# Moving the Wv projection and the transposes of x1 on TensorE in a GCN and graph attention kernel

## Chip, cores, metric

One core of one Trainium2 chip. The metric is the device time of one launch in microseconds, correct against the reference. Kernels are compared in rounds on the same chip.

## The reference, cut to what matters

64 graphs of 256 nodes with 512 features, float32. Two layers, each with a residual and a layer norm:

```python
# layer 0: three graph convolutions
h = relu(adj @ (x @ W1) + b1)
h = relu(adj @ (h @ W2) + b2)
x1 = layernorm(x + adj @ (h @ W3) + b3)
# layer 1: graph attention with one weight per node
q, k = split(x1 @ Wqk); v = x1 @ Wv
w = softmax(mask * sum(q * (adj @ (k * mask)), -1) / sqrt(512))   # over the nodes
out = layernorm(x1 + w[:, :, None] * v)
```

## The kernel before

It works on pairs of graphs in a software pipeline: while pair i goes through layer 0, pair i-1 goes through the end of layer 0 and through the attention. A 512x512 projection takes seven products of half size in place of eight (a Strassen scheme); the sums of the left side are made by VectorE and GpSimd. Wq and Wk are folded into one matrix Wm. A scheduler orders the instructions of each engine; the order of the source is only its starting point.

```python
def left(src, own, eng1, eng2, name, bufs=1):     # sums ahead of a projection
    ...
    eng1.tensor_tensor(S1, A21, A22, op=OP.add)
    eng2.tensor_tensor(S3, A11, A21, op=OP.subtract)
    eng1.tensor_tensor(S2, S1, A11, op=OP.subtract)
    eng2.tensor_tensor(S4, A12, S2, op=OP.subtract)

def seven(lf, w, dst, nodes_out):                 # X, Y, W, Z are PSUM banks
    # X = A11 B11; Y = A12 B21; X += S2 T2; W = S3 T3; X += S1 T1; Z = S4 B22; W += A22 N4
    # ScalarE copies X after the 1st, 3rd and 5th product, VectorE makes the four results
    ...

def load_rest(i):
    ...
    nc.sync.dma_start(xt, xn[i])
    ...
    nc.gpsimd.tensor_tensor(xt..., xt..., bl3..., op=OP.add)      # the bias add, L72

def layernorm(x, g):
    ...
    nc.vector.tensor_scalar(x[:, g, h, :], ..., op0=OP.subtract, op1=OP.mult)   # the scaling, L191

for i in range(NP + 1):
    new = i < NP
    if new:
        s = project(lx, w1, "s", 2)                          # W1
    if prev is not None:
        xt, an = rest
        layer0_out(prev, aTs[i - 1], xt)                     # pp, and the norm of layer 0: x1
    if new:
        ...
        hT = aggregate_relu(s, aTs[i], bl1)                  # pz: first adj product
    if prev is not None:
        x1T = transpose_x1(xt)                               # px: 16 transposes, 4 copies by ScalarE
    if new:
        s = project(left(hT, False, V, PL, "ch"), w2, "s", 2)    # h W2
        ...
    if prev is not None:
        l1 = left(x1T, True, V, PL, "c1")
        ...
        seven(l1, wm, ...)                                   # Wm -> yT
    if new:
        hT = aggregate_relu(s, aTs[i], bl2)                  # pz: second adj product
    if prev is not None:
        w = scores(i - 1, yT, x1T, an)                       # pg
    if new:
        s = project(left(hT, False, V, PL, "ch"), w3, "s", 2)    # h W3
    if prev is not None:
        sm = softmax_rows(w)                                 # pw
        v = project(l1, wv, "vs", 1)                         # x1 Wv
        layer1_out(i - 1, xt, v, softmax_cols(sm))           # ps; weighted v, norm, store
    if new:
        rest = load_rest(i)
    ...
    prev = s
```

## Time and profile before

| | before |
|---|---|
| time, median of 3 | 2982.35 us (2980.95 to 2983.51) |
| TensorE busy | 98% of the span |
| weight loads / VectorE / GpSimd / ScalarE busy | 82 / 46 / 23 / 22% |
| mean granted clock of TensorE, as a share of full speed | 0.996 |
| pass from pp to pp, mean of 29 | 91.57 us |

The page's busy shares say that TensorE is the bound. They do not say what it loses; for that one needs the list of TensorE's waits and the distance between equal points of the timeline. The prediction shows these lines.

How to read them: PE is TensorE's matmuls, PEld its weight loads, DVE VectorE, ACT ScalarE, POOL GpSimd. Numbers are left out of the program's names (c is c1; bx, by, bw, bz are the banks X, Y, W, Z), and x16 means 16 records. [0.53 <-DVE xt L191] means that the engine stood idle for 0.53 us until that instruction released it. An eviction copies a result out of PSUM, where the products are written. A pass is one turn of the loop, measured from pp to pp; the tail is what runs after the last pp.

### The profile page before, as it was taken

How to read it: one execution, taken by the hardware profiler on the slowest of the kernel's cores; microseconds unless marked ns; L12 is line 12 of the kernel's file. 1: busy time of each engine (PE TensorE's matmuls, PEld its weight loads, DVE VectorE, ACT ScalarE, POOL GpSimd, SP SyncE). 2: the span in 40 equal slices, each digit the busy share in tenths (PEclk: the TensorE clock that was granted, in tenths of full speed). 3: DMA queues.
4: the chain of work that ended last, by engine and by line, in shares of the span. 5: the costliest groups of instructions: out<-in, count | busy, mean ns of one | idle time of the engine just before them, and what ended most of it. 6: DMA issues, size and time to landing. Idle time of an engine off the chain costs nothing.

```text
span 2980.8 us, 32161 instructions
## 1 busy us (share of the span) xinstructions
PE 2926.8 (98%) x13216; PEld 2442.2 (82%) x13216; DVE 1363.5 (46%) x2386; ACT 661.5 (22%) x1130; POOL 698.1 (23%) x426
## 2 busy tenths in 40 slices
PE   8999999999999999999999999999999999999997
PEld 6788888888888888888888888888888888888885
DVE  3355334554345543455543455434555345554344
ACT  1222122222222222222212222222222122221221
POOL 4222022221222221222202222112222122221210
PEclk9999999999999999999999999999999999999998
DMA  5011101111011110111110111101111011111000
GB/s 195 22 61 61 46 25 57 53 61 60 11 60 50 60 61 26 45 57 54 60 54 18 60 50 60 61 11 60 50 61 60 32 39 57 53 60 50 8 29 28
DMA packets 33010, 151.29 MB, mean 51 GB/s; under 512 B 3680, under 2 KB 7904, under 8 KB 20320
## 3 DMA queue, kind: packets, MB, share of 16 engines
q1 hardware_dynamic: 32864, 149.24, 13.6%
q8 instruction: 104, 1.70, 0.2%
q14 instruction: 42, 0.34, 0.0%
HBM read 115.68 MB, written 33.55 MB: 50 GB/s over the span
## 4 chain that ended last, share of the span: by engine, by line
PE 90%; DVE 8%; DMA 1%; issue 1%; ACT 1%; POOL 0%; SPq 0%; DVEq 0%; POOLq 0%
PE bx L123 28%; PE bw L123 18%; PE pz L175 10%; PE bz L123 9%; PE by L123 9%; PE pg L223 7%; PE pp L199 6%; DVE xt L191 5%; DVE st L184 1%; PE px L212 1%; DVE xt L201 1%; DMA w<-in_W 1%; PE pt L302 0%; DMA xt<-in_xn 0%; DVE mv L185 0%
## 5 line engine op out<-in xcount | busy, mean ns | idle before, releaser
L175 PE MATMUL pz<-aT,s 128*128 128x256 f32 x2048 | 453.6, 379 | 0.0
L175 PEld LDWEIGHTS pz<-aT,s 128*128 128x128 f32 x2048 | 389.7, 190 | 66.7 <-issue 14.8
L109 POOL TENSOR_TENSOR hT<-hT 128x512 f32<-128x512 f32 x64 | 113.0, 1766 | 880.9 <-DVE ch L108 880.9
L108 POOL TENSOR_TENSOR cx<-xT 128x512 f32<-128x512 f32 x32 | 40.6, 1269 | 1024.9 <-DMA xT<-in_xT 990.0
L191 DVE TENSOR_SCALAR xt<-xt,mv,rs 128x512 f32<-128x512 f32 x256 | 276.8, 1123 | 1.2
L177 ACT ACTIVATE hT<-pz,bl 128x512 f32<-128x512 f32 x256 | 175.2, 685 | 400.8 <-PE pz L175 400.7
L123 PE MATMUL bw<-w,hT 128*128 128x256 f32 x1024 | 242.0, 379 | 1.6 <-POOL hT L109 1.6
L123 PE MATMUL bx<-w,ch 128*128 128x256 f32 x1024 | 242.0, 379 | 0.0
L153 DVE TENSOR_TENSOR s<-bw,t 128x512 f32<-128x512 f32 x96 | 66.4, 692 | 361.9 <-ACT t L152 361.9
L141 ACT COPY u<-bx 128x512 f32<-128x512 f32 x160 | 93.6, 585 | 612.7 <-PE bx L123 612.7
L223 PE MATMUL pg<-x1T,yT 128*128 128x256 f32 x1024 | 226.2, 379 | 0.0
L199 PE MATMUL pp<-s,aT 128*128 128x512 f32 x512 | 225.1, 592 | 0.0
L123 PEld LDWEIGHTS bw<-w,hT 128*128 128x128 f32 x1024 | 189.5, 190 | 33.4 <-POOL hT L109 2.0
L123 PEld LDWEIGHTS bx<-w,ch 128*128 128x128 f32 x1024 | 194.5, 190 | 26.6 <-issue 0.2
L223 PEld LDWEIGHTS pg<-x1T,yT 128*128 128x128 f32 x1024 | 194.6, 190 | 26.5
L152 ACT COPY t<-bx 128x512 f32<-128x512 f32 x160 | 93.6, 585 | 454.7 <-PE bx L123 447.4
L199 PEld LDWEIGHTS pp<-s,aT 128*128 128x128 f32 x512 | 97.2, 190 | 108.8 <-issue 107.1
L147 ACT COPY v<-bx 128x512 f32<-128x512 f32 x160 | 93.6, 585 | 406.5 <-PE bx L123 406.5
L184 DVE BATCH_NORM_STATS2 st<-xt 128x6 f32<-128x512 f32 x256 | 170.6, 688 | 2.1
L72 POOL TENSOR_TENSOR xt<-xt,bl 128x2048 f32<-128x2048 f32 x32 | 145.4, 4544 | 53.5 <-DMA xt<-in_xn 53.5
L108 DVE TENSOR_TENSOR ch<-hT 128x512 f32<-128x512 f32 x64 | 43.9, 686 | 234.5 <-ACT hT L177 234.5
L75 POOL TENSOR_TENSOR an<-an,mr 128x512 f32<-128x512 f32 x64 | 79.8, 1267 | 209.5 <-DMA an<-in_adjn 202.4
(108 smaller groups left out, 4543.2 us busy)
## 6 DMA issues: line engine op xcount, KB each, us to landing
xT<-in_xT SPq DMA_DIRECT2D x32, 1024.0 KB, 4.8
xt<-in_xn SPq DMA_DIRECT2D x32, 1024.0 KB, 6.9
out<-xt SPq DMA_DIRECT2D x32, 1024.0 KB, 3.9
aT<-in_adjT SPq DMA_DIRECT2D x32, 512.0 KB, 3.4
an<-in_adjn SPq DMA_DIRECT2D x32, 512.0 KB, 3.5
mr<-in_mask_row SPq DMA_DIRECT2D x32, 256.0 KB, 3.1
w<-in_W SPq DMA_DIRECT2D x9, 256.0 KB, 6.4
qT<-in_WqT SPq DMA_DIRECT2D x1, 1024.0 KB, 6.9
```

Source lines behind the costliest of these rows:

```text
L72: nc.gpsimd.tensor_tensor(xt.rearrange("p g h d -> p (g h) d"), xt.rearrange("p g h d -> p (g h) d"), bl3.unsqueeze(1).to_broadcast([P, G ...
L109: eng2.tensor_tensor(S3, A11, A21, op=OP.subtract)
L123: nc.tensor.matmul(bank[:, o], lhsT=lhsT, rhs=rhs, start=first and n == 0, stop=last and n == 3, skip_group_check=True)
L141: nc.scalar.copy(u, X)
L147: nc.scalar.copy(v, X)
L152: nc.scalar.copy(t, X)
L175: nc.tensor.matmul(pz[:, g, :], lhsT=s[:, g, m, f * P:(f + 1) * P], rhs=aT[:, g, m, :], start=(m == 0), stop=(m == NH - 1))
L177: nc.scalar.activation(hT[:, f], pz, AF.Relu, bias=bias[:, f:f + 1])
L184: nc.vector.bn_stats(st[:, h, :], x[:, g, h, :])
L191: nc.vector.tensor_scalar(x[:, g, h, :], x[:, g, h, :], mv[:, h, 0:1], rs[:, h:h + 1], op0=OP.subtract, op1=OP.mult)
L199: nc.tensor.matmul(pp, lhsT=aT[:, g, m, h * P:(h + 1) * P], rhs=s[:, g, m, :], start=(m == 0), stop=(m == NH - 1))
L223: nc.tensor.matmul(pg[:, h, :], lhsT=yT[:, d, g, h * P:(h + 1) * P], rhs=x1T[:, d, g, :], start=(d == 0), stop=(d == DC - 1))
```

## The change

The intent: x1 Wv of a pair is put off by one pass and placed between the first adj product and h W2, and the transposes of x1 are placed behind h W2. Both put other TensorE work between pp, whose result the layer norm needs, and the transposes, which need the norm.

```diff
-    prev = None
-    for i in range(NP + 1):
+    def attention_out(i, l1, xt, w):
+        sm = softmax_rows(w)
+        v = project(l1, wv, "vs", 1)
+        layer1_out(i, xt, v, softmax_cols(sm))
+    prev, late = None, None
+    for i in range(NP + 2):
         ...
             hT = aggregate_relu(s, aTs[i], bl1)
-        if prev is not None:
-            x1T = transpose_x1(xt)
+        if late is not None:
+            attention_out(*late)
+            late = None
         if new:
             s = project(left(hT, False, V, PL, "ch"), w2, "s", 2)
             ...
         if prev is not None:
+            x1T = transpose_x1(xt)
+        if new:
+            hT = aggregate_relu(s, aTs[i], bl2)
+        if prev is not None:
             l1 = left(x1T, True, V, PL, "c1")
             ...
         if new:
-            hT = aggregate_relu(s, aTs[i], bl2)
+            s = project(left(hT, False, V, PL, "ch"), w3, "s", 2)
         if prev is not None:
             w = scores(i - 1, yT, x1T, an)
-        if new:
-            s = project(left(hT, False, V, PL, "ch"), w3, "s", 2)
-        if prev is not None:
-            sm = softmax_rows(w)
-            v = project(l1, wv, "vs", 1)
-            layer1_out(i - 1, xt, v, softmax_cols(sm))
+            late = (i - 1, l1, xt, w)
         ...
-        prev = s
+        prev = s if new else None
```

So the diff moves two things more than its title says: the second adj product now stands ahead of Wm, and the scores stand behind h W3.

## The prediction

> **What bounds the kernel now.** I read the page first: busy time by engine.
>
> ```profile
> span 2980.8 us, 32161 instructions
> PE 2926.8 (98%) x13216; PEld 2442.2 (82%) x13216; DVE 1363.5 (46%) x2386; ACT 661.5 (22%) x1130; POOL 698.1 (23%) x426
> ```
>
> TensorE is the bound and nothing else comes near: VectorE is at 46%. The change adds and removes no arithmetic, so it can only win what TensorE waits for. The list of waits, restricted to TensorE, is next (columns: total us, times, longest).
>
> ```profile
> PE px L212 <- DVE xt L191: 19.3, 30, 1.5
> PE bx L123 <- DMA w<-in_W: 7.3, 1, 7.3
> PE px L212 <- issue: 5.8, 1, 5.8
> ```
>
> Only one wait recurs: the transposes of x1 (px) wait for the layer norm of layer 0 (xt, the scaling at L191). The weight load and the 5.8 us are once each, at the start and in the tail. The 19.3 us understate the loss, because ends of matmuls are modelled and the pipeline restarts after each gap. So I took the TensorE timeline (start, us, what) and measured whole passes, from one adj product pp to the next. The first pass has no wait, the others do:
>
> ```profile
> 93.33 7.03 PE L199 MATMUL pp<-s,aT 128*128 128x512 f32 x16
> 107.11 1.91 PE L212 MATMUL px<-ident,xt 128*128 128x128 f32 x16
> ...
> 183.75 7.03 PE L199 MATMUL pp<-s,aT 128*128 128x512 f32 x16
> 197.52 1.04 PE L212 MATMUL px<-ident,xt 128*128 128x128 f32 x8
> 199.09 1.44 PE L212 MATMUL px<-ident,xt 128*128 128x128 f32 x8 [0.53 <-DVE xt L191]
> ...
> 1557.27 7.03 PE L199 MATMUL pp<-s,aT 128*128 128x512 f32 x16
> 1571.04 1.15 PE L212 MATMUL px<-ident,xt 128*128 128x128 f32 x9
> 1573.38 0.98 PE L212 MATMUL px<-ident,xt 128*128 128x128 f32 x7 [1.19 <-DVE xt L191]
> ...
> 2839.40 7.03 PE L199 MATMUL pp<-s,aT 128*128 128x512 f32 x16
> ```
>
> The pass without a wait takes 183.75 - 93.33 = 90.42 us. The 29 passes from 183.75 to 2839.40 take 2655.65 us, 91.57 each. So a pass loses 1.15 us, although the wait itself reads 0.5 to 1.5.
>
> Why is xt late? The VectorE and GpSimd timelines of the same pass show it:
>
> ```profile
> 1568.00 5.32 DVE L191 TENSOR_SCALAR xt<-xt,mv,rs 128x512 f32<-128x512 f32 x2
> ```
> ```profile
> 1568.33 4.71 POOL L72 TENSOR_TENSOR xt<-xt,bl 128x2048 f32<-128x2048 f32 x1
> ```
>
> Two scalings that take 0.97 us elsewhere take 5.32 here, for as long as GpSimd adds the bias to the next x. The last scaling ends at about 1573.3 and the second half of the transposes starts at 1573.38.
>
> The last part is the tail, where the last pair has only its attention left:
>
> ```profile
> 2917.61 7.13 PE L199 MATMUL pp<-s,aT 128*128 128x512 f32 x16
> 2930.55 1.95 PE L212 MATMUL px<-ident,xt 128*128 128x128 f32 x8 [5.81 <-issue]
> 2933.04 1.94 PE L212 MATMUL px<-ident,xt 128*128 128x128 f32 x8 [0.54 <-DVE xt L191]
> 2935.02 3.03 PE L123 MATMUL bx<-x1T,wm 128*128 128x256 f32 x8
> ```
>
> Here nothing hides the layer norm: TensorE stands still for 5.8 + 0.5 us.
>
> **What the Trainium skill says.** "Perfetto Trace Analysis", section Identifying the Most-Contended Engine, warns that matmul busy time is no measure of closeness to roofline. The trace agrees in that 98% hides 1.15 us per pass; gaps and pass lengths tell more. The same page, section Optimization Strategy, says a gap that repeats can mean too few buffers; here the trace differs, the releaser is a VectorE result. "TensorE: Matmul & The Clock Gate", section Step-by-step: what each phase is for, says that only weight loads are pulled ahead and matmuls stay in program order. The trace agrees: W2, ready behind the waiting transposes, doesn't overtake them. So order on TensorE matters, which is what this change edits. "GPSIMD Engine Reference", in its specification table, says its SBUF interfaces are shared with VectorE, with contention for 2-port modes or two inputs from SBUF; the 5.32 against 0.97 us agrees.
>
> **The change part by part.** The built instruction order gives, per steady pass on TensorE: W1, pp, first adj product, row softmax transposes, Wv of the pair before last, column softmax transposes, W2, px, second adj product, Wm, W3, scores. From the timeline: a seven-product projection is 7 x 1.727 = 12.1 us, pp and each adj product 6.9, the scores 6.9, px 1.74 when unhindered, the two softmax transposes 0.4 with a slower matmul behind the second (1.92 for 1.73).
>
> *Removed:* the px wait. Counting from the start of W1, px now stands at 12.1 + 6.9 + 6.9 + 0.2 + 12.1 + 0.4 + 12.1 = 50.7 us; xt was ready at 1573.3 - 1545.1 = 28.2 even with the collision. The slack is 22 us. So 29 x 1.15 = 33.4 us go.
>
> *Added in a steady pass:* nothing on TensorE: as many matmuls as before. On VectorE, layer1_out (1545.8 to 1553.7, 7.9 us) moves from beside W1 to beside W2. The order on VectorE puts the sums ch for W2 ahead of the Wv evictions, so W2 has them (about 28 us) before it starts (38.6).
>
> *The tail.* Before, from pp at 2917.61 to Wm at 2935.02 are 17.4 us for 6.9 + 1.7 of work: 8.8 lost, and 1.1 more in the slow first Wm product (3.03 for 1.89). After, Wv of the last pair but one lies between pp and px and hides the norm. In exchange layer1_out stands on VectorE ahead of the sums c for Wm. From the last Wv eviction I count 0.69 + 2 x 0.64 scaled adds + 4 x 0.6 statistics + 0.5 small + 1.0 scaling before c, 1.25 for its first sum, and with the remaining scaling and second sum 8.6 us; TensorE has 0.8 + 3 x 1.73 = 6.0 us of work that does not need it (7 transposes and three products). About 2.7 us of wait. Net gain 8.8 + 1.1 - 2.7 = 7, of which I take 6.5. The Wv that the tail gains is the one that pass 1 no longer has, so it cancels.
>
> *Sum:* 2982.35 - 33.4 - 6.5 = 2942 us, 1.3% less.
>
> **The rivals.**
>
> *The second adj product waits for W2.* Before, Wm (12 us) lay between; now only 1.74 us of transposes. It needs the last eviction of W2. In the old trace the last eviction of W1 runs from 1557.47 to 1558.16, when the next TensorE instruction started at 1557.27: 0.9 us. Margin 0.85 us. Against it: the transposes are known to be ready and VectorE has finished layer1_out by 47.5 us. If VectorE were late here, 31 passes would lose up to 1 us each and the gain would be eaten: about 2970.
>
> *x comes back too late.* The two xt buffers now live half a pass longer: out is stored only after layer1_out (47.5 us), then xt is loaded, then GpSimd adds the bias, and in GpSimd's order this add stands ahead of the sums for W3. Medians from issue to landing are 3.9 and 6.9 us, so the add starts at about 59 and ends at 63.6; the first W3 sum follows by 65.4. W3 starts at 71.5 and its GpSimd sum is used in the fourth product, 76.6. Slack 11 us, so I expect no wait. If stores and loads took three times as long, each us beyond costs 31 us.
>
> *VectorE holds W2.* If the Wv evictions and layer1_out stood ahead of ch, W2 would wait some 8 us per pass, 250 us in all, clearly slower. The built order says no.
>
> *The collision goes anyway.* In the new order the bias add lies 30 us later, so the normalisation is early for a second reason. That changes no number: the wait is gone either way. But it means that part of the gain could be had without the reordering.
>
> **Range and chances.** The steady-state loss is measured, not guessed, so the centre is firm: even if the tail gains nothing the result is 2949, and with small new waits of 0.3 us per pass 2951 to 2958. On the other side only the tail can give more, 3 or 4 us. Range 2934 to 2960. Over 2% faster would need 2923, more than all waits of TensorE together; over 2% slower needs a new wait of more than 3 us in each pass, which needs one of the margins above to be wrong by 8 us or more. Faster 0.02, within 2% 0.95, slower 0.03.
>
> **What would show it right or wrong.** Right: px no longer among TensorE's waits; passes from pp to pp of 90.4 us; the scaling at L191 (one line further down) without records of 4.7 us; the GpSimd bias add beside the second adj product and Wm; the tail with a wait of 2 to 3 us at the third or fourth Wm product. Wrong: a wait of the second adj product for VectorE in every pass, a wait of W3's products for GpSimd, or passes longer than 90.8 us.

## The result

2942.28 us (2942.27 to 2942.82) against 2981.67 us (2980.95 to 2983.51) in the same rounds: ratio 0.9867, interval 0.985 to 0.9885, 1.3% less.

In the changed kernel all line numbers are one higher (L192 for L191). Its page, span and busy time:

```profile
span 2940.5 us, 32156 instructions
PE 2911.3 (99%) x13216; PEld 2439.0 (83%) x13216; DVE 1286.7 (44%) x2386; ACT 658.9 (22%) x1130; POOL 673.5 (23%) x426
```

VectorE's busy time fell by 77 us with the same 2386 instructions: the 256 scalings fell from 276.8 to 177.6 us, as their records no longer hold the time in which they stood still beside the bias add, and others that now meet GpSimd rose (the first sums ch, at L108, from 43.9 to 73.0 us). TensorE's list of waits (columns: total us, times, longest):

```profile
PE bx L124 <- DMA w<-in_W: 7.3, 1, 7.3
...
PE bx L124 <- DVE c L111: 1.8, 1, 1.8
...
PE bx L124 <- ACT x1T L214: 0.9, 1, 0.9
```

px is gone from it, and nothing that is left occurs more than once. The TensorE timeline (start, us, what):

```profile
171.01 7.03 PE L200 MATMUL pp<-s,aT 128*128 128x512 f32 x16
...
209.59 1.91 PE L213 MATMUL px<-ident,xt 128*128 128x128 f32 x16
...
2792.56 7.03 PE L200 MATMUL pp<-s,aT 128*128 128x512 f32 x16
```

All 16 transposes run in one piece, in every pass but the last. 29 passes take 2621.55 us, 90.40 each. VectorE's timeline in a middle pass, and GpSimd's:

```profile
1533.67 2.65 DVE L192 TENSOR_SCALAR xt<-xt,mv,rs 128x512 f32<-128x512 f32 x2
...
1538.43 1.00 DVE L192 TENSOR_SCALAR xt<-xt,mv,rs 128x512 f32<-128x512 f32 x2
```
```profile
1571.75 4.53 POOL L73 TENSOR_TENSOR xt<-xt,bl 128x2048 f32<-128x2048 f32 x1
1576.91 1.78 POOL L110 TENSOR_TENSOR hT<-hT 128x512 f32<-128x512 f32 x1 [0.63 <-DVE ch L109]
```

The last two scalings take 1.00 us where they took 5.32. (The first two, 2.65 us, run beside GpSimd's sums cx, as they did before.) The bias add now runs 33 us after them. The tail, on TensorE:

```profile
2870.87 7.03 PE L200 MATMUL pp<-s,aT 128*128 128x512 f32 x16
...
2888.76 1.20 PE L213 MATMUL px<-ident,xt 128*128 128x128 f32 x9
...
2893.40 1.99 PE L124 MATMUL bx<-x1T,wm 128*128 128x256 f32 x8 [0.94 <-ACT x1T L214]
...
2900.63 1.97 PE L124 MATMUL bx<-c,wm 128*128 128x256 f32 x8 [1.78 <-DVE c L111]
```

The 5.8 us wait ahead of px is gone; two small ones take its place.

The difference of the spans adds up. 29 passes give 2655.65 - 2621.55 = 34.1 us. The second pp comes at 171.01 in place of 183.75, 12.7 us earlier, as the first pass of the pipeline has no Wv. From the last pp to the end it is 69.6 us in place of 63.2, 6.4 more, as that Wv comes now. Sum: 34.1 + 12.7 - 6.4 = 40.4, against 2980.8 - 2940.5 = 40.3.

### The profile page after: what moved, and what is told of

Same layout as the page of the kernel before. It is cut to its first block, busy times and chain, and to the rows that moved or that the text cites. A ratio compares the mean times of both kernels' runs of the same rounds, so it can differ in the third digit from the quotient of the medians.

```text
span 2940.5 us, 32156 instructions
## 1 busy us (share of the span) xinstructions
PE 2911.3 (99%) x13216; PEld 2439.0 (83%) x13216; DVE 1286.7 (44%) x2386; ACT 658.9 (22%) x1130; POOL 673.5 (23%) x426
## 4 chain that ended last, share of the span: by engine, by line
PE 98%; DVE 1%; DMA 1%; issue 0%; POOL 0%; SPq 0%; DVEq 0%; POOLq 0%
PE bx L124 28%; PE bw L124 19%; PE pz L176 15%; PE bz L124 9%; PE by L124 9%; PE pg L224 8%; PE pp L200 7%; PE px L213 2%; DMA w<-in_W 1%; PE pt L303 0%; PE pw L237 0%; PE ps L252 0%; DVE xt L260 0%; DVE st L185 0%; DVE xt L192 0%
## 5 line engine op out<-in xcount | busy, mean ns | idle before, releaser
L110 POOL TENSOR_TENSOR c<-x1T 128x512 f32<-128x512 f32 x32 | 40.7, 1273 | 725.3 <-ACT x1T L214 725.3
L192 DVE TENSOR_SCALAR xt<-xt,mv,rs 128x512 f32<-128x512 f32 x256 | 177.6, 735 | 1.2
L109 DVE TENSOR_TENSOR ch<-hT 128x512 f32<-128x512 f32 x64 | 73.0, 1141 | 171.0 <-ACT hT L178 171.0
```

Of the source, the lines that this page charges most:

```text
L192: nc.vector.tensor_scalar(x[:, g, h, :], x[:, g, h, :], mv[:, h, 0:1], rs[:, h:h + 1], op0=OP.subtract, op1=OP.mult)
```

## The experiments

The theory: TensorE loses 1.15 us per pass to px's wait for the norm, and the norm is late because of the bias add beside it. The rivals: it is the delay of Wv, or the place of the transposes, that makes the gain, and the collision or the new neighbours of the moved stages do not matter.

### The transposes alone (px_alone)

From the kernel before:

```diff
-        if prev is not None:
-            x1T = transpose_x1(xt)
         if new:
             s = project(left(hT, False, V, PL, "ch"), w2, "s", 2)
         ...
         if prev is not None:
+            x1T = transpose_x1(xt)
             l1 = left(x1T, True, V, PL, "c1")
```

> The transposes of x1 alone move behind W2; Wv and the order after it stay as in the kernel before. Theory (TensorE waits for the norm, and whoever needs x1T must be covered too): the px wait goes, since px now stands 38 us after the start of W1 and xt is ready at 28. But Wm then follows px directly and needs the third of four copies out of PSUM, each 0.59 us behind a bank that fills in 0.43 us: a new wait of TensorE for ScalarE of 0.5 to 1.1 us per pass. Passes of 91.0 to 91.5 us, 2965 to 2980 us in all. Rival (only the place of the transposes counts): passes of 90.4 us, 2949 us.

Measured: 2971.69 us (before 2983.01; ratio 0.9962), passes of 91.15 us. TensorE in a middle pass:

```profile
1303.15 1.91 PE L212 MATMUL px<-ident,xt 128*128 128x128 f32 x16
1305.40 1.99 PE L123 MATMUL bx<-x1T,wm 128*128 128x256 f32 x8 [0.34 <-ACT x1T L213]
```

The wait for the norm is gone, and a new one takes most of its place: Wm follows px at once and waits for ScalarE's copies. It reads 0.34 us, but Wm starts 2.25 us after px where 1.75 are needed: 0.5 us. Its first product then takes 0.1 us more than the pace of 1.73 us (the next starts at 1307.23). That makes 0.6 of the 0.65 us by which this pass (91.07 us) is longer than one without a wait. As expected, freeing px is not enough, its reader needs cover too.

### The change without the delay of Wv (px_no_late)

```diff
         if new:
             s = project(left(hT, False, V, PL, "ch"), w3, "s", 2)
         if prev is not None:
             w = scores(i - 1, yT, x1T, an)
-            late = (i - 1, l1, xt, w)
+            sm = softmax_rows(w)
+            v = project(l1, wv, "vs", 1)
+            layer1_out(i - 1, xt, v, softmax_cols(sm))
```

(against the changed kernel, and `attention_out` is not called)

> The whole change without the delay of Wv: px behind W2, then the second adj product, Wm, W3, scores, and Wv in the same pass. Theory: px is covered by W2, Wm by the second adj product, so passes of 90.4 us and the tail as before: 2982 - 33 = 2949 us, 6 to 8 us above the changed kernel. Rival (the delay of Wv makes the gain): no gain, 2975 to 2982 us.

Measured: 2953.89 us (ratio 0.9902), passes of 90.57 us, the tail's 5.8 us wait as before. So most of the gain needs no delay of Wv. But it is 5 us more than expected, 0.15 us per pass. VectorE and TensorE of one pass:

```profile
1281.42 4.24 DVE L191 TENSOR_SCALAR xt<-xt,mv,rs 128x512 f32<-128x512 f32 x2
...
1286.29 0.69 DVE L110 TENSOR_TENSOR ch<-ch,hT 128x512 f32<-128x512 f32 x1
```
```profile
1285.33 1.89 PE L123 MATMUL by<-w,hT 128*128 128x256 f32 x8
1287.12 1.97 PE L123 MATMUL bx<-w,ch 128*128 128x256 f32 x8
```

Here the bias add is still beside the norm, VectorE's sums ch for h W2 stand behind the stretched scalings, and the product that reads them starts 1.79 us after the one ahead of it, where 1.73 is the pace, and lasts 0.08 longer: 0.14 us. That reading was tested by the next variant.

### The same, with the bias add later (px_no_late_add_later)

```diff
+        with tc.issue_after(behind.ins):      # behind: GpSimd's last sum of x1T
             nc.gpsimd.tensor_tensor(xt..., xt..., bl3..., op=OP.add)
```

> The change without the delay of Wv, and with the bias add of the next x behind GpSimd's sums of x1T. Theory (the 5 us that this variant lost against its expected 2949 are W2's third product waiting 0.15 us per pass for VectorE's sums, which stand behind the scalings stretched by the bias add): passes fall from 90.57 to 90.4 us and the time to 2949 us. Rival (the split row-softmax transposes cost the 0.15 us): 2954 us, no change.

Measured: 2948.30 us (ratio 0.9884), passes of 90.41 us. The 5 us were the stretched scalings, by way of ch.

### Wv delayed alone (wv_alone, wv_alone_again)

Against the changed kernel:

```diff
         if late is not None:
             attention_out(*late)
             late = None
+        if prev is not None:
+            x1T = transpose_x1(xt)
         if new:
             s = project(left(hT, False, V, PL, "ch"), w2, "s", 2)
         ...
-        if prev is not None:
-            x1T = transpose_x1(xt)
-        if new:
-            hT = aggregate_relu(s, aTs[i], bl2)
         if prev is not None:
             l1 = left(x1T, True, V, PL, "c1")
             ...
+        if new:
+            hT = aggregate_relu(s, aTs[i], bl2)
```

> Wv delayed alone: it stands behind the first adj product, px stays directly ahead of W2 and Wm ahead of the second adj product as before. Theory: px starts at 38.6 us after W1 with xt ready at 28, so no wait; W2 covers the copies for Wm; the tail gains as in the changed kernel: passes of 90.4 us and 2942 us, the same as with the whole change. Rival (the place of the transposes behind W2 is needed): the px wait stays, about 2975 us.

Measured: 2941.39 us (ratio 0.986), passes of 90.37 us, no wait for px. Here the bias add has moved as well (it starts at 1299.28, 31 us behind the last scaling), so this run does not tell the cover by Wv from the end of the collision. px_no_late and add_later do: in the first the collision stays, with scalings of up to 4.74 us, and in the second the old order of TensorE stays. To compare it with the changed kernel it ran once more, in the same rounds:

> Wv delayed alone, again, in the same rounds as the changed kernel: 2941.4 us, 0.5 to 1 us below the changed kernel; all theories alike.

> The changed kernel, as the measure for the other three: 2942.3 us; all theories alike.

2941.41 us (2941.27 to 2941.56) against 2942.22 us (2942.11 to 2942.83). Wv alone does all that the change does, and is 0.8 us faster. So the move of the transposes adds nothing once Wv stands ahead of them. Where the 0.03 us per pass come from was not looked into.

### No transposes between h W2 and the second adj product (pz2_behind_w2)

As wv_alone, but the second adj product stays ahead of Wm:

```diff
         if new:
             s = project(left(hT, False, V, PL, "ch"), w2, "s", 2)
         ...
-        if prev is not None:
-            x1T = transpose_x1(xt)
         if new:
             hT = aggregate_relu(s, aTs[i], bl2)
```

(against the changed kernel; `transpose_x1` stands behind `attention_out`)

> As the changed kernel, but px ahead of W2, so that the second adj product stands directly behind W2 with no transposes between. Theory (the 1.74 us of transposes cover W2's last eviction): TensorE waits for the eviction in each pass, 0.9 us after the matmul plus restart, about 1 us times 31: 2970 to 2976 us, and the list of waits names the second adj product and the eviction of bw. Rival (the eviction is in time anyway): 2942 us.

Measured: 2946.44 us (ratio 0.9879), passes of 90.54 us: 0.17 us more than with Wv alone, not 1 us. This was a miss in size. The weight loads of one pass:

```profile
1297.48 0.84 PEld L176 LDWEIGHTS pz<-aT,s 128*128 128x128 f32 x4
1298.64 1.38 PEld L176 LDWEIGHTS pz<-aT,s 128*128 128x128 f32 x7 [0.32 <-DVE s L159]
```

The wait is there, for the eviction named. But four loads go ahead of it: the built order puts two matmuls that read the first half of s, one for each graph, in front (two records each), and at 0.216 us per record these are 0.86 us of cover. So the product has its own cover for nearly all of the 0.9 us.

### The bias add alone (add_later)

The kernel before, with the edit of px_no_late_add_later and no other. TensorE's stages are in the old order.

> The kernel before with one instruction moved: the bias add of the next x on GpSimd is queued behind GpSimd's sums of x1T, so it no longer runs beside the scalings of the norm. TensorE's order is untouched. Theory (the collision makes xt late): the two scalings take about 1 us in place of 5.3, xt is ready at about 24 us after the start of W1 and px at 26 no longer waits: passes of 90.4 us, tail as before, 2949 us. Rival (VectorE's queue is late anyway): the px wait stays above 0.3 us per pass, 2965 to 2982 us.

Measured: 2948.78 us (before 2982.59; ratio 0.9886), passes of 90.41 us ((2805.36 - 183.54) / 29). VectorE, GpSimd and TensorE in a middle pass:

```profile
1279.87 1.00 DVE L192 TENSOR_SCALAR xt<-xt,mv,rs 128x512 f32<-128x512 f32 x2
```
```profile
1290.17 4.52 POOL L73 TENSOR_TENSOR xt<-xt,bl 128x2048 f32<-128x2048 f32 x1
```
```profile
1282.09 1.91 PE L213 MATMUL px<-ident,xt 128*128 128x128 f32 x16
```

One GpSimd instruction gives 33.8 of the change's 40 us. In the pass that the prediction shows, it started 2.7 us ahead of px (1568.33 against 1571.04); here it starts 8.1 us behind px (1290.17). The norm now ends 1.2 us before px starts. So the collision was the cause of the steady wait; VectorE's queue alone is in time. What is missing to the changed kernel is the tail. "SBUF — State Buffer", section Who interferes with whom, says that whoever of VectorE, in a 2-port mode, and GpSimd issues first holds the ports they share for its whole instruction and that the other blocks until then. The trace agrees: in the kernel before, the two scalings last until 1573.32, the add until 1573.04. That a scaling runs in such a mode is not shown by a trace.

### VectorE's sums behind layer1_out (sums_behind_out)

Against the changed kernel:

```diff
         if new:
-            s = project(left(hT, False, V, PL, "ch"), w2, "s", 2)
+            with tc.issue_after(done.ins):    # done: the last scaling of layer1_out
+                lh = left(hT, False, V, PL, "ch")
+            s = project(lh, w2, "s", 2)
```

> The changed kernel with VectorE's sums ch for W2 forced behind layer1_out, which is the order of the source. Theory (VectorE's order is what makes the delayed Wv free): ch is ready only about 49 us after the start of W1 while W2's third product could start at 42: a wait of about 7 us in 30 passes, 3140 to 3170 us, slower than both kernels. Rival (a few us on VectorE don't matter): 2942 us.

Measured: 3234.53 us (ratio 1.0846), beyond the expected 3140 to 3170; passes of 100.14 us, 9.74 more. TensorE, and the table of stretches of the same pass (us busy of each engine, then PEclk, the granted clock):

```profile
1310.35 1.22 PE L124 MATMUL bw<-w,hT 128*128 128x256 f32 x2 [7.40 <-POOL hT L110]
1311.36 3.32 PE L124 MATMUL bx<-w,ch 128*128 128x256 f32 x8
```
```profile
core 0: us, PE busy (x) PEld busy (x) DVE busy (x) ACT busy (x) POOL busy (x), PEclk, DMA share, GB/s
1290.00:1300.00 10.00, 10.00 (x49) 8.46 (x48) 2.92 (x6) 1.17 (x2) 0.00 (x0) 1.00 0.00 0
...
1310.00:1313.40 3.40, 3.05 (x7) 2.52 (x8) 0.00 (x0) 0.00 (x0) 1.52 (x2) 0.50 0.59 176
...
1316.80:1320.00 3.20, 3.20 (x17) 2.73 (x16) 1.23 (x2) 0.58 (x1) 3.20 (x1) 1.00 0.00 0
```

The wait is 7.4 us, as expected. The rest, 2.2 us in this pass of 99.97 us, is nearly all the clock: after the gap it is granted at 0.50, and the first ten records take 4.16 us (to 1314.51) where the pace of 0.216 us each gives 2.16. "TensorE: Matmul & The Clock Gate", section What's actually happening, gives half the clock after an idle window of some 3.4 us, and the full one again after a busy window of that length; the trace agrees, with 0.50 after a gap of 7.4 us and 1.00 again some 4 us after the restart at 1310.35 (in windows of 1 us: 0.50 up to 1314, 0.88 up to 1315, then 1.00). So the order on VectorE that the scheduler chose, against that of the source, carries the change.

### The tail (tail_sums_first, after_again, wv_alone_tail)

In the changed kernel's last pass but one, layer1_out of the last pair but one was queued on VectorE behind the sums for Wm.

```diff
+        if owed is not None:                  # the last pair but one
+            with tc.issue_after(sums.ins):    # VectorE's second sum for Wm
+                layer1_out(*owed)
```

> The changed kernel, in its last pass but one with the sums for Wm ahead of layer1_out on VectorE. Theory (1.8 us of the tail's wait is layer1_out standing ahead of the sums): the wait of the Wm product for c goes, the 0.9 us wait for the copy of x1T stays: 1.5 to 2.5 us less than the changed kernel, 2940 us. Rival (the wait moves on to the GpSimd sums or to layer1_out at the end): no change.

> The changed kernel again, on the same chip and in the same rounds as the others: 2942 us, all theories alike.

Measured: 2941.93 us (2941.89 to 2942.04) against 2942.36 us (2942.05 to 2942.54) of the changed kernel in the same rounds: 0.4 us. The rival was right in that the wait moved on, though not to a place that it named. TensorE's timeline:

```profile
2905.75 1.99 PE L124 MATMUL bw<-x1T,wm 128*128 128x256 f32 x8 [1.80 <-DVE yT L154]
```

The wait of 1.8 us moved on to an eviction of Wm, which now stands behind layer1_out. So layer1_out went behind the evictions as well, on top of Wv alone:

```diff
-            with tc.issue_after(sums.ins):
+            with tc.issue_after(last.ins):    # the last eviction of yT
                 layer1_out(*owed)
```

> Wv delayed alone, and for the last pair but one layer1_out queued on VectorE behind all four evictions of Wm. Theory (the 1.8 us wait of the tail went over to the eviction of yT when layer1_out was put between the sums and the evictions): with both ahead of it the wait is gone and only the 0.9 us wait for the copy of x1T stays: 1.5 to 2 us less than Wv alone, 2939.5 us. Rival (it moves on once more, to the products of the scores): no change.

Measured: 2939.00 us (2938.94 to 2939.02), 2.4 us below Wv alone and 3.2 below the changed kernel in the same rounds; ratio to before 0.9853. In its list of waits only the 0.9 us for the copy of x1T is left of the tail. It is the fastest of all that ran.

## Why the prediction was right, point by point

- **The bound, and the loss per pass.** Right. The pass without a wait (90.42 us) forecast the new pass (90.40 us). The matmuls' records of the wait, 18.8 us in these 29 passes, would have given little more than half of the 34.1 us. The prediction overlooked a line further down in the whole list of waits, that of the weight loads:

```profile
PEld px L212 <- DVE xt L191: 33.6, 54, 1.7
```

All 54 waits lie in the 29 passes. They sum up to nearly the whole loss, and in 26 of the passes they agree with the pass's own loss within 0.05 us. In 25 passes the weight loads wait twice (in the first of them 0.77 us, then after one transpose 0.32 us more), and the second wait does not show between the matmuls, whose ends are modelled.
- **The collision as the cause of the late norm.** Right, and shown by add_later: without it px does not wait even in the old order. The prediction held that only part of the gain could be had so; it is 33.8 of 40 us.
- **Nothing added in a steady pass.** Right: no wait of TensorE between 270 and 2750 us. It rests on VectorE's order, as sums_behind_out shows with 292 us. The prediction put that rival at 250 us, with 8 us of wait per pass (measured 7.4); the term that it lacked is the clock after the gap.
- **The margin of 0.85 us at the second adj product.** Mis-sized, without harm, in the term for the cover of the last eviction: pz2_behind_w2 has no transposes there and loses only 0.17 us per pass, as two matmuls of the product can run before the eviction. The true margin is about 0.86 us larger.
- **The return of x.** Right: the bias add starts 56.8 us after the start of W1 (1571.75 - 1514.90), where 59 were estimated, and the sum for h W3 ends at 1578.7, 12.8 us before its product at 1591.48 (estimated slack 11).
- **The tail.** Right in sum: 6.3 us gained (12.7 - 6.4), 6.5 taken. The expected wait of 2.7 us at Wm came as 1.78 us for VectorE's sums and 0.94 us for ScalarE's copies, which the prediction had not listed. So the wait foretold was 0.9 us too long, and that a wait of that size came elsewhere is luck.
- **Which part of the change works.** The prediction gave the removal of the wait to both moves together. The runs split it: the delay of Wv alone gives all of it; the transposes behind h W2, with the second adj product behind them, give 29 us (2953.89), and 11 when Wm follows at once (2971.69). With the bias add out of the way they add nothing to speak of (2948.30, against 2948.78 for the add alone, in different rounds).
- **A reading.** The matmul behind the second softmax transpose takes 1.83 us to the next start (1545.08 to 1546.91), not 1.92. It changes nothing: px stands 50.7 us after the start of W1, as foretold (1565.56 - 1514.90).

## What to carry to other kernels

On an engine that is 98% busy, measure the distance between equal points of passes with and without the wait: it tells the loss better than the matmuls' own records of the wait. Read the weight loads' waits beside them: here they came to 33.6 of 34.1 us, though in pz2_behind_w2 they read 0.32 us a pass for a loss of 0.17. Before reordering stages, ask what makes the awaited result late; here one instruction on a mostly idle engine, moved by some 10 us, gave most of the gain. When a stage moves, look at three places: what it waits for, what now follows it at once, and the order that the scheduler makes of the other engines' work.

## What the Trainium skill lacked or had wrong

- "TensorE: Matmul & The Clock Gate", section Part 4: PE-mode transpose: it gives the duration of one bf16 transpose (about 275 ns within a kernel; 273 ns here, in float32), not the pace in a row: 16 of them take 1.75 us, 109 ns each.
- "Perfetto Trace Analysis", section Optimization Strategy: it sends one to the gaps between records, and does not say that on TensorE the gap between matmuls can be smaller than the loss, nor to look at the weight loads' gaps. Here 18.8 us of waits of matmuls and 33.6 us of waits of weight loads stood for 34.1 us of time, and in px_alone 0.34 us of record for 0.6 us.
- The same section: a gap that repeats can mean too few buffers for the next tile, and no other cause is named for it there, though the paragraph before it sends one to the releaser, which led to the cause here. Here the buffers stayed as they were, and moving one GpSimd instruction ended it (33.8 us).
